# Rewriting the edges of a graph layer behind 60 plain groups instead of 100

## The chip, the cores and the metric

The kernel runs on one core of a Trainium2 chip. The metric is the device time of one execution in microseconds (us). The core has five engines that matter here: PE (TensorE, matmuls), DVE (VectorE), ACT (ScalarE), POOL (GpSimd, which issues the indirect gathers) and SP (SyncE, which issues the plain DMAs). Each runs its own instructions in order, and semaphores make one wait for another.

## The reference

It is one layer of a graph network on 50000 nodes and 1650000 directed edges, sorted by destination `dst`; 50000 of the edges are self loops. Each node has 160 numbers (64 scalars, 32 vectors of 3), each edge four weights. Cut to what matters:

```python
ss, vv = s[src], v[src]                       # gather of x rows by source
out0, out1 = products of (ss, vv) with edge weights e0, e1 and W1 to W5
m_agg = jax.ops.segment_sum(m, dst, num_segments=n)
h  = concatenate([m_agg[:, :64] @ Ws * LIN_S, einsum('nui,uw->nwi', m_agg_v, Wv) * LIN_V])
x  = layernorm(x + (x + relu(h)))
```

As everything up to the relu is linear in the gathered rows, the kernel sums `weight k of the edge × gathered row` by destination first, for k = 0 to 3, and multiplies the sums by combined matrices after.

## The kernel before

**Groups and pairs.** Edges are taken 128 at a time (a unit), 6 units to a group (G = 6), two groups to a pair (PG = 2), 20 groups (SG), so ten pairs, to a load. There are 2087 groups, in 1044 pairs and 105 loads.

**What a pair does.** POOL gathers 12 × 128 rows of `x` into one of four `xg` buffers (line 319; the pool is opened with `bufs=4`). DVE writes `hot` (line 328: which of 32 destinations each edge has, as 0 and 1) and `ha` (line 331: `hot` times each of the four weights). PE multiplies (line 343, `ps`), and DVE transposes the result in 32 × 32 squares (line 349, `sums`). Every two pairs, PE multiplies by the weights (line 579, `phc`) and ACT copies the result out (line 581, `hp`). For each block of 128 nodes PE adds up the groups that touch it (line 639, `phb`), and the node's own term is made (lines 615 to 629: `xt` read at 592, the self loop's weights `sa` read at 596, `ptx`, `xT`, `yx`, `t`). Lines 184 to 199 are the layer norm, 735 sends `out`.

**What a load does.** `load(s)` is called at every tenth pair for the next ten: the plain one reads `src` and `dst` (`ri`) and the weights (`ra`) on SP (lines 260 to 262). One pair later ACT casts them (line 269). Four pairs later `place(s)` (lines 284 to 311) works out where each group begins (`first`, `baseB`), transposes the indices and the weights on PE (lines 285 to 301) and writes `si` (line 303, what the gathers read), `rel` and, in PSUM, `pk` (what `ha` reads).

**Rewriting.** The first HEAD groups are read plainly, self loops with them. For all later edges the self loops are taken out of the stream first, since the node's own term needs no gather. That is done in packs: a pack holds 128 rows of 790 edges, and is a list of 128 steps (function `pack`, some of them empty): read the rows (SP, lines 419 to 423, 2.4 MB), cast them (ACT, lines 427 to 429 and 447), count and mark the self loops and examine the marks (DVE, lines 448 to 493), then two series of shifts by powers of two with predicated copies (DVE, lines 504 to 511, each in two half rows): one gathers the weights of the self loops in `pra`, then lines 523 to 528 pick and collect them into `mine`; the other closes the gaps in the rows, `prow`. Last, SP puts the rows into DRAM one by one (line 563, one DMA of 18.5 KB to `edges` and one of 0.5 KB to `selves` a row). Later loads read from `edges` (line 254, `r6`, 360 KB), and `sa` comes from `selves`.

**What sets the order.** SP's instructions keep the order in which the program is written (`manual_schedule` for SP). Those of the other engines are arranged by a scheduler when the program is built, and are then fixed. A pack's steps are dealt out over the pairs, so that it is done `(first - 1) * per - 1` pairs in, where `first` is the first load that needs its rows and `per` is 10:

```python
todo = math.ceil(len(packs[0]) * min(1, (p + 1 - began) / max(1, due[0] - began)))
```

Pack 0 begins at pair 2 (START). With HEAD = 100 it is due at pair 39; the next ones at 99, 159 and 229. There are 16 packs.

Of the kernel before, what the change touches and what calls it, by code (L numbers as in the profile page):

```python
# [67 lines left out]
SG = 20  # L68

HELP = {}  # L70
HEAD = 100
RP = 128
RS = 16
KM = 31
# [4 lines left out]
def plan(n_nodes, n_edges):  # L79
# [9 lines left out]
                if g == 1 or (g + 0.2) * per_unit + 1 + 5 * math.sqrt(g * per_unit * per_unit / P) <= W)  # L89
    head = math.ceil(min(HEAD, n_edges / (group * P)) / SG) * SG  # L90
    eh = head * group * P
# [917 lines left out]
```

## Time and profile before

| | |
|---|---|
| median of 3 runs | 15705.15 us (15704.62 to 15706.36) |
| the profiled execution | 15737.51 us, span 15735.7 us |
| POOL busy | 11891.8 us, 76% |
| PE busy | 8152.5 us, 52% |
| DVE busy | 6035.6 us, 38% |
| first gather, last gather start | 9.82 us, 15716.99 us |
| mean granted TensorE clock | 0.73 |

How to read it: an engine's busy time leaves out the issuing of DMAs and the handling of semaphores, so a POOL that does nothing but gathers has 76%; the rest stands as "issue" in its waits. A group of instructions reads "line engine operation output<-inputs, shape, count | busy us, mean ns of one | idle time of the engine just before them, and what ended it". A timeline row has start and duration in us, engine (SPq is the queue of SP), line, operation, names and, in square brackets, an idle time before and what ended it. DVE rows that don't wait for one another overlap slightly in the records.

Some times of pairs in that execution, in us from the start of the span:

| pair | gathers, first start to last end | transpose (line 349) |
|---|---|---|
| 14 | 233.95 to 248.67 | 255.85 |
| 15 | 248.98 to 263.69 | 288.30 |
| 16 | 264.00 to 278.71 | 302.15 |
| 19 | 309.09 to 323.81 | 332.12 |
| 20 | 324.11 to 338.86 | 348.69 |
| 46 | 715.07 to 729.80 | 763.85 |

Pair 30's first gather starts at 474.52, pair 50's at 775.23.

### The profile page before, as it was taken

Reading aid. Unit: us, or ns where it says so; the run is one execution under the profiler, and the core shown is the slowest. Engines: PE = TensorE matmul, PEld = TensorE weight load, DVE = VectorE, ACT = ScalarE, POOL = GpSimd, SP = SyncE. Lnnn points to the kernel's source line nnn. Section 1 sums busy time; section 2 is a strip of 40 time slices with the busy share of each in tenths; the row PEclk is TensorE's granted clock in tenths of the full one; section 3 lists DMA queues with packets and bytes.
Section 4 is the critical chain, followed back from the end, with each engine's and each line's share of the span. In section 5 each row is a group of like instructions: output and inputs, shape, how many; then the busy total and the mean of one; then the engine's idle time right before and its main releaser. Section 6 shows DMA issues by size and latency. Waiting matters only on the chain. (4 is left out here: it accounts for less than half of the span.)

```text
span 15735.7 us, 122013 instructions
## 1 busy us (share of the span) xinstructions
PE 8152.5 (52%) x38505; PEld 7452.0 (47%) x38506; DVE 6035.6 (38%) x11070; ACT 499.5 (3%) x1392; POOL 11891.8 (76%) x12536
## 2 busy tenths in 40 slices
PE   4554545555455555555455554554545555455555
PEld 4444545444454444444444444454444444444444
DVE  5342524325253342533425343352433425234222
ACT  0000000000000000000000000000000000000000
POOL 7777777777777777777777777777777777777777
PEclk7777777777777777777777776777777777777777
DMA  3323333233233323333233332332333332332232
GB/s 79 84 74 84 75 76 80 74 82 75 76 80 77 80 75 76 80 78 79 73 79 78 77 81 74 83 75 75 80 76 81 75 82 73 76 79 73 73 75 68
DMA packets 806901, 1215.93 MB, mean 77 GB/s; under 512 B 280851, under 2 KB 585160, under 8 KB 802278
## 3 DMA queue, kind: packets, MB, share of 16 engines
q0 software_dynamic: 601056, 1026.60, 26.6%
q1 hardware_dynamic: 203770, 180.19, 3.9%
q8 instruction: 323, 5.29, 0.1%
q14 instruction: 312, 2.56, 0.1%
q10 hardware_dynamic: 1440, 1.29, 0.0%
HBM read 1135.77 MB, written 71.40 MB: 77 GB/s over the span
## 5 line engine op out<-in xcount | busy, mean ns | idle before, releaser
L319 POOL DMA_INDIRECT xg<-in_x,si x12522 | 11887.6, 949 | 3825.5 <-issue 3777.2
L343 PE MATMUL ps<-xg,ha 128*128 128x160 f32 x25044 | 5686.4, 408 | 7298.0 <-DMA xg<-in_x,si 5676.0
L343 PEld LDWEIGHTS ps<-xg,ha 128*128 128x128 f32 x25044 | 5451.3, 281 | 7580.6 <-issue 6593.5
L349 DVE STREAM_TRANSPOSE sums<-ps 128x320 f32<-128x320 f32 x1044 | 530.7, 512 | 6311.9 <-PE ps L343 6240.0
L331 DVE TENSOR_TENSOR ha<-hot,pk 128x1536 f32<-128x1536 f32 x1044 | 1802.6, 1730 | 206.3 <-PE ps L343 206.3
L627 DVE TENSOR_SCALAR t<-yx,sa 128x160 f32<-128x160 f32 x391 | 147.5, 377 | 2585.8 <-PE yx L623 2585.5
L623 PE MATMUL yx<-BWh,xT 80*128 80x320 f32 x3128 | 1032.0, 472 | 156.6 <-ACT xT L617 152.7
L579 PE MATMUL phc<-BWk,sums 128*128 128x160 f32 x5220 | 820.6, 305 | 22.2 <-DVE t L629 19.7
L623 PEld LDWEIGHTS yx<-BWh,xT 80*128 80x128 f32 x3128 | 599.3, 202 | 439.2 <-ACT xT L617 237.4
L579 PEld LDWEIGHTS phc<-BWk,sums 128*128 128x128 f32 x5220 | 750.7, 193 | 49.6 <-issue 40.3
L639 PE MATMUL phb<-hp,hot 128*128 128x160 f32 x3474 | 562.0, 307 | 6.1 <-DVE t L629 4.3
L328 DVE TENSOR_TENSOR hot<-bank,rel 128x384 f32<-128x384 f32 x1044 | 551.1, 540 | 0.1
L639 PEld LDWEIGHTS phb<-hp,hot 128*128 128x128 f32 x3474 | 503.1, 194 | 60.5 <-issue 50.4
L629 DVE SCALAR_TENSOR_TENSOR t<-yx,sa,t 128x160 f32<-128x160 f32 x1173 | 442.6, 377 | 82.4 <-PE yx L623 67.8
L511 DVE COPY_PREDICATED prow<-marks,prow 128x2370 f32<-128x2370 int32 (+8 forms) x160 | 442.5, 2765 | 0.0
L617 ACT COPY xT<-ptx 80x256 f32<-80x256 f32 x391 | 143.8, 368 | 8133.7 <-PE ptx L615 8133.3
L581 ACT COPY hp<-phc 128x160 f32<-128x160 f32 x522 | 150.3, 288 | 5316.5 <-PE phc L579 5284.5
L511 DVE COPY_PREDICATED pra<-marks,pra 128x1580 f32<-128x1580 int32 (+8 forms) x160 | 304.5, 1903 | 0.0
L605 DVE TENSOR_TENSOR hot<-bank,rr 128x512 f32<-128x512 f32 (+2 forms) x391 | 285.3, 730 | 0.0
L640 DVE TENSOR_TENSOR phb<-phb,t 128x160 f32<-128x160 f32 x391 | 127.4, 326 | 136.1 <-PE phb L639 134.4
L615 PE MATMUL ptx<-ident,xt 128*80 128x128 f32 (+1 forms) x782 | 154.5, 278 | 38.4 <-ACT hp L581 34.1
L193 ACT ACTIVATE rstd<-mv,eps_t 128x1 f32<-128x1 f32 x391 | 115.2, 295 | 1707.3 <-DVE mv L188 1630.5
(144 smaller groups left out, 2600.6 us busy)
## 6 DMA issues: line engine op xcount, KB each, us to landing
xg<-in_x,si POOLq DMA_INDIRECT x12522
edges<-prow SPq DMA_DIRECT2D x1994, 18.5 KB
r<-edges SPq DMA_DIRECT2D x99, 360.0 KB
selves<-mine SPq DMA_DIRECT2D x1992, 0.5 KB
xt<-in_x SPq DMA_DIRECT2D x390, 80.0 KB
out<-o SPq DMA_DIRECT2D x390, 80.0 KB
pra<-in_attr SPq DMA_DIRECT2D x15, 1580.0 KB
sa<-selves SPq DMA_DIRECT2D x390, 2.0 KB
```

The source lines that it names most:

```text
L319: got.append(nc.gpsimd.indirect_dma_start(out=xg[:, j, :], out_offset=None, in_=x, in_offset=bass.IndirectOffsetOnAxis(ap=placed[0][:, u + ...
L328: nc.vector.tensor_tensor(hot[:, :n], slotsP[:, 0:W].unsqueeze(1).to_broadcast([P, n, W]), rel[:, u:u + n].unsqueeze(2).to_broadcast([P, n ...
L331: nc.vector.tensor_tensor(ha[:, :n], hot[:, :n].unsqueeze(2).to_broadcast([P, n, NK, W]), pk[:, :, u:u + n].rearrange("p k u -> p u k").un ...
L343: mm = nc.tensor.matmul(ps[:, j // G, :], ha[:, j].rearrange("p k w -> p (k w)"), xr, start=j % G == 0, stop=j % G == G - 1)
L349: nc.vector.transpose(at[:, :, i:i + ng, :].rearrange("p b g w -> p g b w"), ps[:, :ng].rearrange("p g (b f) -> p g b f", f=FB))
L511: nc.vector.copy_predicated(what[:n, a:e], mi[:, r].unsqueeze(2).to_broadcast([n, e - a, what.shape[2]]), what[:n, a + d:e + d])
L579: nc.tensor.matmul(ph[:ng * W], at[:, b, :ng].rearrange("p g w -> p (g w)"), BWk[:, b, :], start=b == 0, stop=b == ND - 1)
L605: nc.vector.tensor_tensor(hot2[:, :len(cs)], slotsP.unsqueeze(1).to_broadcast([P, len(cs), P]), rr[:, :len(cs)].unsqueeze(2).to_broadcast( ...
L615: nc.tensor.transpose(pt[:, i, :nb], xt[:nb, i * H:(i + 1) * H], ident[:nb, :nb])
L623: nc.tensor.matmul(y[:nb], xT[:, i, :nb], BWh[:, i, ks, :], start=i == 0, stop=i == 1)
L629: nc.vector.scalar_tensor_tensor(t[:nb], y[:nb, i], sa[:nb, k:k + 1], t[:nb], op0=ALU.mult, op1=ALU.add)
L639: nc.tensor.matmul(ph[:nb], hot2[:r, i, :nb], hp[:r], start=i == 0, stop=i == len(cs) - 1)
```

## The change

The constant HEAD goes from 100 to 60.

```diff
-HEAD = 100
+HEAD = 60
```

With it `plan()` gives 60 plain groups instead of 100, so three plain loads instead of five and 102 `r6` loads instead of 100; 2033 rows to rewrite instead of 1994, still in 16 packs; 2086 groups instead of 2087, so 12516 gathers instead of 12522 (the self loops of the plain groups are gathered with the rest: about 46080/33 = 1396 instead of 76800/33 = 2327). Pack 0 is due at pair 19 instead of 39 and has 18 pairs instead of 38; the next ones are due at pairs 79, 139 and 209. Line 563 makes 4319 DMAs instead of 4236.

In the order of the built program, DVE's instructions are the same up to the transpose of pair 14. In the program before, the half-steps of pack 0's shifts then alternate with the `hot`, `ha` and transposes of pairs 15 to 22. In the changed one, all that is left of pack 0 at the transpose of pair 15 (the end of the first series of shifts, lines 523 to 528, the second series) follows that transpose without anything between, and `place(2)` and the `ha` of pair 16 come after it. On SP, `load(2)` (lines 260 to 262) stood ahead of pack 0's puts and now stands behind the first 16 of them, which is where `load(3)` stood. `place(3)` reads an `r6`, which stands on SP behind all of pack 0's puts and behind pack 1's reads, and on DVE behind the first half of pack 1's count (lines 448 to 469).

## The prediction

> **What bounds the kernel now.** I read the page first, then POOL's waits, then the DVE, SP and PE timelines around the first pack. From the page:
>
> ```profile
> span 15735.7 us, 122013 instructions
> ...
> L319 POOL DMA_INDIRECT xg<-in_x,si x12522 | 11887.6, 949 | 3825.5 <-issue 3777.2
> ```
>
> 12522 gathers with 0.949 us of work and 0.30 us of issue each make 1.2528 us apiece, 15688 of the 15736 us. POOL's waits, as us in total, times, longest:
>
> ```profile
> POOL xg L319 <- issue: 3777.2, 12389, 0.4
> POOL xg L319 <- DMA xg<-in_x,si: 17.4, 53, 0.8
> POOL xg L319 <- DVE rel L306: 6.8, 1, 6.8
> ```
>
> So nothing in the body stops POOL: time is the number of gathers by 1.2528, plus any stall of POOL. It has four `xg` buffers, so the gather of pair p+4 waits for the last matmul of pair p (line 343), and that waits for pair p's `ha` on DVE (331). What counts is whether DVE can leave that chain alone.
>
> In DVE's timeline pack 0's steps now alternate with the chain (start, us, instruction):
>
> ```profile
> 305.69 0.58 DVE L509 COPY_PREDICATED pri<-marks,pri 128x395 int32<-128x395 int32 x1
> 306.17 2.86 DVE L511 COPY_PREDICATED prow<-marks,prow 128x2370 f32<-128x2370 int32 x1
> 308.93 0.50 DVE L349 STREAM_TRANSPOSE sums<-ps 128x320 f32<-128x320 f32 x1
> 309.36 0.54 DVE L504 TENSOR_SCALAR marks<-pri 128x395 int32<-128x395 int32 x1
> ...
> 361.68 2.67 DVE L511 COPY_PREDICATED prow<-marks,prow 128x2274 f32<-128x2274 int32 x1
> ```
>
> The last L511 ends at 364.35; SP, which waited for it, then puts the rows out, with the next plain load behind 16 puts:
>
> ```profile
> 133.00 0.40 SPq L260 DMA_DIRECT2D ri<-in_src  x1
> ...
> 364.42 0.30 SPq L563 DMA_DIRECT2D edges<-prow  x1
> ...
> 370.77 0.35 SPq L260 DMA_DIRECT2D ri<-in_src  x1
> 371.18 0.43 SPq L261 DMA_DIRECT2D ri<-in_dst  x1
> 372.03 0.32 SPq L262 DMA_DIRECT2D ra<-in_attr  x1
> ```
>
> The load at 133.00 is that of groups 40 to 59 (pairs 20 on), the one at 370.77 that of pairs 30 on.
>
> **The change, part by part.**
>
> *Gathers.* The plan gives 2086 groups instead of 2087: 12516 gathers, 6 fewer by 1.2528, −7.5 us. The tail after the last gather (15716.99 to 15735.7, 18.7 us) stays.
>
> *Other counts.* Two plain loads become `r6` loads; 39 more rows are put (83 more SP DMAs of 0.23 us, over 16 packs); the packs' casts and DVE steps stay 16 times. POOL issues none of these; later packs keep 60 or 70 pairs each. Nothing for these, while SP's longest put stretch, priced below, stays ahead.
>
> *Pack 0 in 18 pairs instead of 38.* Its 128 steps go out 7.1 a pair instead of 3.4, and the built order shows where: up to the transpose of pair 14 DVE's order is that of before; after the transpose of pair 15 comes the rest of pack 0 in one block (three half-steps of the `pra` shift, L523/L525 twice, L528, ten half-steps of `prow`, the last two short), with no `hot`, `ha` or transpose between. Only then come `place(2)` (L284 on) and the `ha` of pair 16. On SP, load(2) now stands behind pack 0's first 16 puts, so behind the block's last L511. Before, it went at 133.00.
>
> The block starts when pair 15's matmuls end:
>
> ```profile
> 265.44 6.26 PE L343 MATMUL ps<-xg,ha 128*128 128x160 f32 x24 [8.54 <-DMA xg<-in_x,si]
> ...
> 286.29 6.08 PE L343 MATMUL ps<-xg,ha 128*128 128x160 f32 x24 [12.41 <-DVE ha L331]
> ...
> 297.31 2.88 PE L343 MATMUL ps<-xg,ha 128*128 128x160 f32 x20
> ```
>
> 271.7, with the transpose 272.2. Its length: a `prow` half-step is L504 0.56, L506 0.55, L508 0.64, L509 0.58, L511 2.77. In the trace dependent neighbours start 0.04 after the end of the one before (L186 to L188, 698.63 + 0.33 to 698.99) and independent ones 0.1 before it (L509 to L511, 306.17). That makes 5.15; a `pra` half-step with L511 at 1.88 makes 4.3. Sum: 3 × 4.3, two picks 4.8 (0.55 + 1.78 each), L528 5.6, 8 × 5.15 = 41.2, last two 6.9: 71.4 us, to 343.6. If all neighbours overlap as in the interleaved stretch it is 65.
>
> Then (tE = the block's end), by before's rows after 364.35: puts from tE+0.07, `ri` at +6.4 and +6.8, `ra` at +7.7; its packets end at 374.0 and 375.1 (+9.7 and +10.8). From there the place(6) stretch is the pattern:
>
> ```profile
> 586.00 0.27 DVE L284 TENSOR_SCALAR first<-starts,rf 120x20 f32<-120x20 f32 x1
> ...
> 589.29 1.74 DVE L331 TENSOR_TENSOR ha<-hot,pk 128x1536 f32<-128x1536 f32 x1
> ...
> 596.72 0.52 DVE L349 STREAM_TRANSPOSE sums<-ps 128x320 f32<-128x320 f32 x1 [1.43 <-PE ps L343]
> ```
>
> ACT's cast (L269) at 585.56 to the matmuls' end at 596.7 is 11.1 us. Pair 16 is done near tE + 9.7 + 11.1 ≈ tE+21, 364.6. Pair 20's gather, which started at 324.11, starts there: a stall of 40.5 us. Pairs 17 to 19 are gathered by then, 3.4 us of matmul each, and the old pace returns. This wait also holds pair 16's `hot`, `ha`, transposes, own terms and `out` behind it; none reaches POOL except through pair 20.
>
> What the trace can't show is a block alone on DVE and matmuls after 80 us of idle PE. Bounds: block 65 to 71.4 (I take 71.4, the dependent row, as each instruction of the order waits for its neighbour); matmuls 3.4 (764.70, warm) to 6.1 (286.29, after idle); I take 5.6. Low end 40.5 − 6.4 − 2.2 ≈ 32; high 41.
>
> Row against rule: PEclk is 0.50 over 126 to 138 us and 1.00 over 138 to 144. The Trainium skill ("TensorE: Matmul & The Clock Gate", Part 1, "What's actually happening") says one idle window of some 3.4 us halves the clock and some 3.4 us of work restores it, so it would price pair 16 at 3.4 cold plus about 1.7 warm, 5.1 us: 0.5 less than my row, and the sum 0.5 lower.
>
> *SP's puts and pair 30.* Pack 0's 17 groups of 16 put DMAs run without a pause from 343.7, with `out` and `xt` between. Before, the first group with the load took 9.3 us (364.42 to 373.75), one alone 7.9 (to 381.63), one with `out` or `xt` some 8.7, the last, short one 5.3 (605.46 to 610.75): 9.3 + 9 × 7.9 + 6 × 8.7 + 5.3 = 138, to 482. Behind them pack 1's 2.4 MB and then `r6` for pair 30: before, that pack's load was issued at 612.16 and landed at 621.8, so `r6` lands near 494. Pack 1's count (L448 to L469 from about 490, 6.6 us as at 732.51) stands ahead of L284 on DVE: 496.6; ten more us to the `ha` of pair 26 (739.07 on, less its `yx` waits), then 3.4 to 6: done at 510.5 to 513. Pair 30's gather is due at 474.52 + 40.5 = 515.0. Margin 2 to 4.5 us, so nothing; the cover is thin, and past it each us is a us of stall.
>
> **Sum**: +40.5 − 7.5 = +33. The profiled execution took 15737.5 (span 15735.7), 32 above the median of 15705.15, without a cause that I can name; its pace of gathers is 0.2% slower, which moves a stall of 40 us by 0.1. After's span on that footing 15769; predicted median 15705 + 33 = 15738.
>
> **Rivals.**
>
> *A, the buffers cover it (the other side).* If pair 16 is done by 324.1, POOL sees nothing: −7.5, 15698. Price: block plus 21 us against 52 (324.1 − 272.2), so no stall needs a block under 31 us, and a block under 38 us breaks even. For it: four buffers hide every wait in the trace. Against: the block's 13 L511, two L525 and L528 alone sum to 42 us.
>
> *B, a second wait at pair 30.* If all puts run at 8.8 us a group (381.63 to 390.47) or `r6` lands late behind the 2.4 MB, pair 26 is 3 to 20 us later and the margin goes: +36 to +55, 15741 to 15760. For: the margin of only 2 to 4.5. Against: pair 46 before, the same place one pack later, was done at 763.85 with its buffer needed at 775.23, 11 us early.
>
> *C, a shorter stall.* Block at the interleaved pace and warm matmuls: 32 − 7.5, so +24 to +28, 15729 to 15733. For: 361.68 to 364.25 shows overlap at work. Against: the waits in the order.
>
> *D, the order is not what runs.* The order is fixed at build, so only data readiness can differ; a gain beyond A has no source.
>
> **How the numbers follow.** 0.2% of 15705, 31.4 us, is about what a measurement here can tell from no change. Forecast (+28 to +36) 0.47, B 0.25, C 0.20, A 0.05, other 0.03. Slower by over 0.2%: B whole, 0.65 of the forecast, a little of other: 0.57. Faster by over 0.2% needs −31 where only 7.5 is to be had: 0.02. Same: 0.41. Range: 15724 (C's end less 5, for a landing or a matmul quicker than any row here) to 15760 (B's end); A is left out.
>
> **What would show it.** In the changed profile: one POOL wait of about 40 us ahead of pair 20's first gather, near 324; DVE from 272 to 344 in L504 to L528 alone; load(2) issued near 350; puts from 344 to 482; no POOL wait near 515; 12516 gathers at 1.25 us. No wait near 324 makes A right; a second one near 515, B; 32 us at the first, C. I am wrong if POOL's pace itself changes (0.2% of it is as much as the whole effect) or the stall is over 60 us.

## The result and the profile after

The changed kernel takes 15747.44 us (median of 10 runs, 15745.27 to 15748.56); before, timed with it, takes 15705.85 us (10 runs, 15703.89 to 15706.82). That is +41.6 us, a ratio of 1.0026 [1.0018, 1.0035]: slower, by a little more than the 31.4 us (0.2%) that the prediction held a measurement to tell from no change; the interval's lower end is just under that. The forecast was 15738, +33.

The profiled execution took 15747.3 us. Its span, gathers and POOL's waits (us in total, times, longest):

```profile
span 15745.5 us, 122127 instructions
...
L319 POOL DMA_INDIRECT xg<-in_x,si x12516 | 11847.6, 947 | 3871.1 <-issue 3768.1
```

```profile
POOL xg L319 <- issue: 3768.1, 12369, 0.3
POOL xg L319 <- PE ps L343: 40.7, 5, 39.4
POOL xg L319 <- DMA xg<-in_x,si: 34.4, 73, 1.4
```

There is one long wait of POOL, 39.4 us for a matmul, which before did not have. The waits for DMA are 34.4 us instead of 17.4, which nobody forecast. The long one is at pair 20's first gather; the row above it in POOL's timeline is pair 19's last:

```profile
322.76 0.94 POOL L319 DMA_INDIRECT xg<-in_x,si  x1 [0.30 <-issue]
363.14 0.94 POOL L319 DMA_INDIRECT xg<-in_x,si  x1 [39.44 <-PE ps L343]
```

What pair 16's matmuls wait for is seen in DVE's timeline:

```profile
270.74 0.52 DVE L349 STREAM_TRANSPOSE sums<-ps 128x320 f32<-128x320 f32 x1 [9.32 <-PE ps L343]
271.18 0.55 DVE L504 TENSOR_SCALAR marks<-hit 128x395 int32<-128x395 int32 x1
...
339.96 2.67 DVE L511 COPY_PREDICATED prow<-marks,prow 128x2274 f32<-128x2274 int32 x1
352.05 0.23 DVE L284 TENSOR_SCALAR first<-starts,rf 120x20 f32<-120x20 f32 x1 [9.42 <-ACT rf L269]
...
362.91 0.52 DVE L349 STREAM_TRANSPOSE sums<-ps 128x320 f32<-128x320 f32 x1 [1.11 <-PE ps L343]
```

Pair 15's transpose, the block of pack 0 from 271.18 to 342.63 with nothing of a pair in it, 9.42 us in which DVE has nothing to do, then `place(2)` and pair 16's transpose. The idle 9.42 us are spent on the load of pair 20's groups, which SP could only issue after the block, in SP's timeline:

```profile
342.70 0.30 SPq L563 DMA_DIRECT2D edges<-prow  x1
...
348.27 0.34 SPq L260 DMA_DIRECT2D ri<-in_src  x1
348.66 0.40 SPq L261 DMA_DIRECT2D ri<-in_dst  x1
349.11 0.41 SPq L262 DMA_DIRECT2D ra<-in_attr  x1
```

Where the 41.6 us lie, from the two profiled executions (the place ahead of each number):

| where | us |
|---|---|
| wait at pair 20's first gather, 39.44 instead of 0.30 | +39.1 |
| 6 gathers fewer, at 1.250 us (0.947 + 0.30) | −7.5 |
| time lost by POOL from pair 900 on, 12.1 instead of 7.2 | +4.9 |
| from the last gather's start to the end, 15722.60 to 15745.5 instead of 15716.99 to 15735.7 | +4.2 |
| first gather, at 10.22 instead of 9.82 | +0.4 |
| sum | +41.1 |

The two executions differ by only 9.8 us, since that of before ran 32 us above its own median: its gathers took 1.2527 us each, and those of the changed kernel 1.2503. Over 12516 gathers this is 30 us, and it is no part of the change: the table's rows are differences of waits, not of starts.

The +4.9 comes from the last pack. SP issues the reads of its rows like this:

```profile
13687.27 17.72 SPq L422 DMA_DIRECT2D pri<-in_dst  x1
13705.03 12.36 SPq L423 DMA_DIRECT2D pra<-in_attr  x1
```

and while the packets of `pra`, one of 12640 bytes a row, move, from 13719.25 to 13782.99, gathers have to wait for theirs, for instance

```profile
13749.75 0.94 POOL L319 DMA_INDIRECT xg<-in_x,si  x1 [1.39 <-DMA xg<-in_x,si]
```

Before, the last pack held 1994 − 15 × 128 = 74 rows, and its packets of `pra` took 20.9 us (13990.08 to 14010.98). Now it holds 2033 − 15 × 128 = 113, and they take 63.7 us, 22 GB/s. A pack of 128 rows, more than either, takes 5.1 to 7.1 us in the two executions. (Of before's 7.2 us, 4.8 are one slow gather, told of in the last section; the last read thus costs 12.1 us now and at most 2.4 before.)

The +4.2 is in the chain of work that ended last. Before:

```profile
15716.99 4.43 DMA xg<-in_x,si
...
15721.45 0.55 PE ps L343 x2
...
15722.43 1.60 PE phc L579 x10
15724.03 1.10 PE phb L639 x8
```

and after:

```profile
15722.60 5.22 DMA xg<-in_x,si
...
15727.86 0.90 PE ps L343 x2
15728.76 1.60 PE phb L639 x6
15730.36 3.43 PE phc L579 x20
15733.79 2.62 PE phb L639 x14
```

2087 groups left one group in the last pair; 2086 leave two, and 20 instead of 10 weight multiplies (579) and 20 instead of 8 sums over groups (639) come after the last gather has landed.

### The profile page after: what moved, and what is told of

It reads as the page before. It is cut to its first block, busy times and chain, and to the rows that moved or that the text cites. A ratio compares the mean times of both kernels' runs of the same rounds, so it can differ in the third digit from the quotient of the medians.

```text
span 15745.5 us, 122127 instructions
## 1 busy us (share of the span) xinstructions
PE 8150.1 (52%) x38497; PEld 7448.5 (47%) x38498; DVE 6047.3 (38%) x11067; ACT 498.8 (3%) x1390; POOL 11851.8 (75%) x12530
## 5 line engine op out<-in xcount | busy, mean ns | idle before, releaser
L511 DVE COPY_PREDICATED prow<-marks,prow 128x2370 f32<-128x2370 int32 (+8 forms) x160 | 442.5, 2765 | 0.1
L511 DVE COPY_PREDICATED pra<-marks,pra 128x1580 f32<-128x1580 int32 (+8 forms) x160 | 305.0, 1907 | 0.0
L605 DVE TENSOR_TENSOR hot<-bank,rr 128x512 f32<-128x512 f32 (+3 forms) x391 | 286.5, 733 | 0.1
```

What stands on the lines that cost most here:

```text
L511: nc.vector.copy_predicated(what[:n, a:e], mi[:, r].unsqueeze(2).to_broadcast([n, e - a, what.shape[2]]), what[:n, a + d:e + d])
L605: nc.vector.tensor_tensor(hot2[:, :len(cs)], slotsP.unsqueeze(1).to_broadcast([P, len(cs), P]), rr[:, :len(cs)].unsqueeze(2).to_broadcast( ...
```

## The experiments

The theory: pack 0's block and, behind it on SP, `load(2)` make the wait at pair 20; its length is the block and some 20 us more, less 52 us that the buffers cover. The main rival: that 18 pairs are simply too few, so that the denser steps delay DVE wherever the load stands. Further open: which lock is next if the buffers are made more, and whether the shape of the last pack costs anything.

The twelve runs, of seven kernels, came in four groups, each on one chip with the kernel before beside it. On three of these chips before itself took 19476 to 19626 us, and in the profiles taken there PE is held back (the last section); totals are compared within a group only, and what a wait does is read from the traces.

**The load put ahead of the puts.** Four empty steps in pack 0 shift its first put behind `load(2)` in SP's order; 60 groups, 18 pairs and all the work stay. DVE's built order changes with it: there is no block between the transposes of pairs 15 and 16 any more, and pack 0's half-steps alternate with pairs 15 to 19.

```diff
             steps += [None, None]
             steps += [None, None]
+            if c == 0:
+                steps += [None] * 4
```

> 60 plain groups, with four empty steps ahead of pack 0's puts, so that load(2) stands on SP ahead of them, as load(2) and load(3) stood with 100. In the built order pack 0's shifts alternate with the ha of pairs 16 to 23 again. Queue theory (the block and the wait at pair 20 come from load(2) standing behind a put that waits for the whole pack; 18 pairs are also too few for the puts): no wait at pair 20; pack 0 ends near 372 us instead of 343, its puts near 509, r6 lands near 521, pair 26 is done near 538 and pair 30's gather, due at 474, waits some 64 us. Time 15747 + 25 = 15772. Rival (only the place of load(2) is at fault): no wait anywhere, 15747 - 39 = 15708. Rival (the density of 7.1 steps a pair alone makes the wait): the wait at pair 20 stays, 15747.

> The kernel of e1_load_ahead again (60 plain groups, load(2) on SP ahead of pack 0's puts), on a chip where PE is not held up. Queue theory: no wait at pair 20; pack 0 ends near 372 us, its puts near 509, r6 lands near 521, pair 26 is done near 538, and pair 30's gather, due at 474, waits some 64 us; 15747 + 25 = 15772. Rival (only the place of load(2) is at fault): no wait anywhere, 15747 - 39 = 15708. Rival (the density of the steps alone): a wait at pair 20 as after has it.

> The kernel of e1_load_ahead and e5_load_ahead, for the chip of the last call, where PE is not held up (before at 15707). Queue theory: no wait at pair 20; pack 0 ends near 372 us, its puts near 509, r6 lands near 521, pair 26 is done near 538, pair 30's gather, due at 474, waits some 64 us: 15747 + 25 = 15772. Rival (only the place of load(2) is at fault): no wait anywhere, 15747 - 39 = 15708. Rival (the density of the steps alone): a wait at pair 20 as after has it, 15747.

It ran in three groups, each time on a chip with PE held back: 19715.07 against 19626.1 (1.0050 [1.0033, 1.0067]), 19584.83 against 19475.77 (1.0052 [1.0035, 1.0069]) and 19715.63 against 19611.87 (1.0069 [1.0044, 1.0094]). POOL's timeline in the first, at pair 20 and at pair 30:

```profile
372.76 0.95 POOL L319 DMA_INDIRECT xg<-in_x,si  x1 [0.30 <-issue]
...
667.00 1.00 POOL L319 DMA_INDIRECT xg<-in_x,si  x1 [98.64 <-PE ps L343]
```

The wait at pair 20 is gone in all three; it is 78.6 us in the kernel with the load behind the puts, in the same group (below). So the density of the steps alone does not make this wait, and that rival falls for pair 20: the place of one load does, together with the order that is built from it (the edit moves both, and no run parts them). But much of the time is then waited for later: 34.2, 34.5 and 34.2 us at pair 26 and 98.6, 96.0 and 96.7 us at pair 30, where pair 30's own load stands behind all of pack 0's puts. The wait at pair 26 is the same lock with the next read in `load(2)`'s place. After the last `ha` before pack 0's end, at 444.44, the shifts run alone to 471.17, and `xt`, which an own term needs, stands on SP behind the puts that wait for them. From SP's and PE's timelines in the first group (in this kernel the lines from 539 on stand 2 further down):

```profile
471.24 0.28 SPq L565 DMA_DIRECT2D edges<-prow  x1
...
486.98 0.38 SPq L594 DMA_DIRECT2D xt<-in_x  x1
```

```profile
489.82 0.62 PE L617 MATMUL ptx<-ident,xt 128*80 128x128 f32 x2 [54.30 <-DMA xt<-in_x]
```

Pair 22's matmuls come behind this `ptx` on PE; its transpose is at 504.20, and pair 26's gather starts at 504.44. In the first group the waits at pairs 26 and 30 are together 53.8 us more than the same two in the other kernel (9.4 and 69.6), of the 78.3 that were saved. In total it is 52.0 us below that kernel (19767.07), where 24.5 are left of these waits; the rest was not followed up. Against before it is still 0.5 to 0.7% slower, so that 18 pairs cost time even with `load(2)` ahead is not refuted. How long pair 30 would wait on a chip whose PE is not held back was not measured.

**A shorter block.** Pack 0 leaves out the first two of its five `prow` shifts, four half-steps (the rows are then not closed up); empty steps keep everything else in place.

```diff
-                for b in range(bits):
+                for b in range(2 if c == 0 and far == "far" else 0, bits):
...
-                steps += [partial(next, g, None)] * (4 * KM.bit_length() - (0 if all_ else 2))
+                steps += [partial(next, g, None)] * (4 * KM.bit_length() - (0 if all_ else 10 if c == 0 else 2))
+                steps += [None] * (8 if c == 0 and not all_ else 0)
```

> 60 plain groups; pack 0 leaves out the first two of five shifts of prow, four half-steps of 5.2 us, so its rows are not closed up rightly. Block theory (the wait is block + 20.3 us less 52): block 71.4 - 20.9 = 50.5, wait at pair 20 of 39.1 - 20.9 = 18.2 us, all after it earlier by as much: 15747 - 21 = 15726. Rival (the wait is set by SP's puts and the load, not by DVE): wait and time as they are, 15747.

> The kernel of e2_short_pack again: 60 plain groups, pack 0 without the first two of five shifts of prow (four half-steps of 5.2 us; its rows are not closed up rightly). Block theory: block 50.5 us, wait at pair 20 of 39.1 - 20.9 = 18.2 us, 15726. Rival (the wait is set by SP's puts and the load): 39 us, 15747.

In the first group its total is 19724.47 against 19626.1 (1.0059 [1.0042, 1.0075]), in the second 19587.46 against 19475.77 (1.0057 [1.0040, 1.0074]). The totals say little, as pair 30's waits of 69.2 and 74.4 us, and PE's pace after them, are in them. The wait itself, in the first group:

```profile
433.42 0.94 POOL L319 DMA_INDIRECT xg<-in_x,si  x1 [56.92 <-PE ps L343]
```

78.62 − 56.92 = 21.7 us less than with the whole block in the same group, where the four half-steps were priced at 20.9. The block itself, from its first L504 to its last L511, is 50.5 us instead of 71.4, so 20.9 less: within 0.8 us, each microsecond of block was a microsecond of wait. In the second group the wait is 46.06 us, with no run with the whole block and four buffers beside it. The length of the wait depends also on how late POOL already is when it begins; the time from the end of pair 15's transpose to pair 20's first gather hardly does. It is 91.9, 93.0 and 92.5 us with the whole block (the changed kernel, the one with the read in two pieces in the first group, and the same where PE keeps its pace), and 71.3 and 70.8 us with the short one.

**A fifth buffer.**

```diff
-tc.tile_pool(name="rows", bufs=4) as rowp
+tc.tile_pool(name="rows", bufs=5) as rowp
```

> 60 plain groups, five xg buffers instead of four. If the wait at pair 20 is for the buffer alone, one more covers a further pair: the wait moves to pair 21 and is 39.1 - 15.0 = 24 us, 15732. If pair 20's own si is also late, as the place(2) at 352.05 to 354.85 suggests, pair 20 waits for that, to 354.9: 30.9 us, 8.2 less, 15739. In before the spare buffer would bring nothing.

> The kernel of e3_five_buffers again: 60 plain groups, five xg buffers. If the wait at pair 20 is for a buffer alone: it moves to pair 21 and is 39.1 - 15.0 = 24 us, 15732. If pair 20's si (ready near 354.9) holds it next: 30.9 us at pair 20, 15739.

19378.89 against 19626.1 (0.9874 [0.9858, 0.9891]) and 19232.28 against 19475.77 (0.9876 [0.9846, 0.9905]). These totals are a gain only on chips where PE is late throughout; they say nothing on the others. At pair 20 the wait is still there, and its releaser is another one. DVE's and POOL's timelines in the first:

```profile
459.08 0.28 DVE L303 TENSOR_SCALAR si<-bank 128x120 int32<-128x120 f32 x1 [0.23 <-issue]
459.28 0.27 DVE L306 SCALAR_TENSOR_TENSOR rel<-bank,baseB 128x120 f32<-128x120 f32 x1
```

```profile
459.63 0.95 POOL L319 DMA_INDIRECT xg<-in_x,si  x1 [88.39 <-DVE rel L306]
```

No buffer is waited for here, but the indices `si` of pair 20, which `place(2)` writes, which waits for the same `load(2)`. From the end of pair 15's transpose to that gather it is 83.6 us, and 93.0 in the kernel with four buffers in the same group: 9.4 less, where 8.2 was expected (83.7 in the second group). So behind the lock of the four buffers stands the next, less than 10 us of wait away.

**Fifth buffer and shorter block together.** Both diffs above.

> 60 plain groups, pack 0 without the first two of five shifts of prow (20.9 us less block; its rows are not closed up rightly), and five xg buffers. Block theory with si as the next lock: si(2), written at 354.8 in after, comes at 333.9, pair 20 waits some 10 us, no wait at pair 21: 15747 - 29 = 15718. If the buffer alone is the lock: no wait at pair 20, 18.2 - 15.0 = 3 us at pair 21, 15711. If the block's length does not set it: 31 us at pair 20, 15739.

19376.99 against 19611.87 (0.9895 [0.9871, 0.9919]).

```profile
439.22 0.94 POOL L319 DMA_INDIRECT xg<-in_x,si  x1 [67.95 <-DVE rel L306]
```

The wait is 88.39 − 67.95 = 20.4 us shorter than with the whole block, though on another chip; with the whole block it was 88.39 and 87.5 us on two chips. From the end of pair 15's transpose to pair 20's first gather it is 63.1 us, against 83.6 and 83.7. So the block sets this second lock one for one too.

**The last read in two pieces.** The reads of a pack (lines 419 to 423) are made in two, the first of a multiple of 16 rows, so 112 and 1 instead of 113.

```diff
+                m = n // 16 * 16
+                for r, q in ((0, m), (m, n)):
+                    if r == q:
+                        continue
+                    e = slice(e0 + r * L, e0 + q * L)
-                dq.dma_start(pri[:n, 0, :L], src1[e].rearrange("(r e) o -> r (e o)", e=L))
+                    dq.dma_start(pri[r:q, 0, :L], src1[e].rearrange("(r e) o -> r (e o)", e=L))
...
-                dq.dma_start(pra[:n, :L].rearrange("r e k -> r (e k)"), attr[e].rearrange("(r e) k -> r (e k)", e=L))
+                    dq.dma_start(pra[r:q, :L].rearrange("r e k -> r (e k)"),
+                                 attr[e].rearrange("(r e) k -> r (e k)", e=L))
```

> 60 plain groups; a pack's reads of pri and pra go out in two pieces, the first of a multiple of 16 rows. Only the last pack differs: 113 rows become 112 and 1. Theory: the read of 113 rows is what slowed the gathers of pairs 911 to 913 by 12.1 us (its 12640 byte packets came one each 0.56 us from 13719.25 to 13782.99, those of 128 rows one each 0.045 us); with 112 + 1 rows it lands within some 8 us and the gathers keep their 1.25 us: 15747 - 11 = 15736. Rival (the slow stretch is a matter of the place in the data or of the moment): it stays, 15747.

> The kernel of e4_even_read again: 60 plain groups, a pack's reads in two pieces. Theory: the slow stretch of 12.1 us at the last pack's read goes (that read took 63.8 us from first to last packet with 113 rows and 6.5 with 112 + 1 in the runs before this one); where PE is not held up 15747 - 11 = 15736, wait at pair 20 as in after, 39 us. Rival (the slow stretch belongs to the place in the data): 15747.

The first of them, in the first group, took 19767.07 against 19626.1 (1.0075 [1.0058, 1.0092]). Its two waits are those that the other kernels of that group are set against:

```profile
451.39 0.94 POOL L319 DMA_INDIRECT xg<-in_x,si  x1 [78.62 <-PE ps L343]
...
694.58 0.94 POOL L319 DMA_INDIRECT xg<-in_x,si  x1 [69.59 <-PE ps L343]
```

The packets of its last read take 7.0 us from the first one's start to the last one's end, and 64.3 to 65.2 us where the read is whole in that group. The second ran on a chip where before takes 15706.85: 15736.62 us (15735.54 to 15738.43), ratio 1.0019 [1.0009, 1.0029], where 15736 was expected. SP's reads of the last pack, and POOL there and at pair 20:

```profile
13684.01 0.42 SPq L427 DMA_DIRECT2D pri<-in_dst  x1
13684.48 0.43 SPq L428 DMA_DIRECT2D pra<-in_attr  x1
```

```profile
364.08 0.94 POOL L319 DMA_INDIRECT xg<-in_x,si  x1 [41.09 <-PE ps L343]
...
13749.92 0.94 POOL L319 DMA_INDIRECT xg<-in_x,si  x1 [0.30 <-issue]
```

SP issues in 0.43 us what took 12.36, no gather waits there, and pairs 911 to 913 lose less than 0.1 us instead of 12.1. They gather the same rows as in the changed kernel, so the place in the data is not the cause. The total is 15747.44 − 15736.62 = 10.8 us below the changed kernel, of another chip, with befores 1.0 us apart. The wait at pair 20 is as long as ever, so the slow read is a term by itself.

**80 groups, with the read in two pieces.** HEAD = 80 gives pack 0 28 pairs, half of the step between the two kernels; at first with four buffers.

```diff
-HEAD = 60
+HEAD = 80
```

> 80 plain groups, and each pack's reads in two pieces, the first of a multiple of 16 rows (the last pack has 93 rows: 80 and 13). Pack 0 has 28 pairs, its puts begin near 380 us, load(3) stands behind half of them, near 447, and pair 26 is done near 463, ahead of pair 30's need at 474.5. Theory: no wait at pairs 20 to 40; 12516 gathers as with 60 groups, 7.5 us less than before; a tail after the last gather of 23 us instead of 18.7 (an even number of groups, the last pair whole), +4.2; no slow stretch in the last pack's read, -6.6 against before: 15706 - 10 = 15696. Rival (a pack in fewer than 38 pairs always stops POOL): a wait of some 20 us, 15716 or more.

19481.88 against 19475.77, 1.0002 [0.9991, 1.0014]. At pair 20 4.4 us are left, but pairs 30 and 40 wait 56.3 and 39.2 us on this chip; that no pair would wait on a chip with PE at its pace was not shown by it.

**80 groups, read in two pieces, five buffers.**

> 80 plain groups, five xg buffers, reads of a pack in two pieces. Where PE is not held up (before at 15706): no wait at pairs 20 to 40, 12516 gathers (-7.5), tail +4.2, last read -6.6: 15696, the fifth buffer brings nothing. Where PE is held up in stretches (before at 19480 to 19630): the fifth buffer covers one more pair of each stretch, as in e7_five_buffers (1.2% under before although that kernel has the waits at pairs 20 and 30); without those waits some 0.5% more, 1.6 to 1.8% under before.

On the chip where before takes 15706.85 (15705.41 to 15710.98), it takes 15698.75 us (15696.31 to 15700.70), where 15696 was expected: 8.1 us less, with no run of the one within the runs of the other, but a ratio of 0.9994 [0.9985, 1.0004], which is no difference by the bound of 31.4 us. It is the fastest kernel here, by an amount that these runs can't vouch for. POOL's waits:

```profile
POOL xg L319 <- issue: 3784.5, 12422, 0.6
POOL xg L319 <- DMA xg<-in_x,si: 15.7, 43, 2.1
```

But for the first gather's 7.3 us for its indices, which before has too (6.8), there is no wait for a matmul or an index left. Its pack 0 was slower than expected (last shift done at 407.05, not 380; `load(3)` at 465.75, not 447): pair 26's transpose starts at 482.57, and pair 30's first gather went at 476.32. With four buffers it would have waited some 6 us (an estimate from these two rows); the fifth covers it.

## Why the prediction was right, and where it was not

The forecast was +40.5 − 7.5 = +33; measured +41.6. That is inside the range of 15724 to 15760, but above the +28 to +36 that the forecast itself covered, in the band set for rival B, whose second wait did not come: in this part the range held by luck. Step by step:

| step | predicted | measured |
|---|---|---|
| block of pack 0 | 71.4 us | 71.45 (271.18 to 342.63) |
| its end tE | 343.6 | 342.63; it began 1.0 sooner, as pair 15's matmuls took 5.24 us instead of 6.26 |
| `ri` of `load(2)` issued | tE + 6.4 and 6.8 | tE + 5.6 and 6.0 |
| ACT's cast | tE + 9.7 | tE + 9.0 |
| pair 16's matmuls | 5.6 us | 5.2 |
| pair 16 done | tE + 21 | tE + 20.2 |
| wait at pair 20 | 40.5 us | 39.4, so 39.1 more than before |
| six gathers | −7.5 | −7.5 |
| pack 0's puts end | 482 | 477.5 |
| margin at pair 30 | 2 to 4.5 us | 4.0 |

The cast is in ACT's timeline, the matmuls that set the margin in PE's:

```profile
351.61 0.40 ACT L269 CAST rf<-ri 120x256 f32<-120x256 int32 x1 [104.91 <-DMA ri<-in_dst]
```

```profile
503.53 5.68 PE L343 MATMUL ps<-xg,ha 128*128 128x160 f32 x24 [4.54 <-DVE ha L331]
```

Pair 26 is done at 503.53 + 5.68 = 509.2, and pair 30's first gather went at 513.22 with no wait. Rival A (the buffers cover the block) was refuted by the wait itself, rival B (a second wait at pair 30) by this margin. That the lock of B is real was seen on the chips where PE is late: there pair 30 waited 69 to 99 us with 60 plain groups and four buffers. Rival C (a shorter block) fell with 71.45 us; the value from neighbours that wait for each other was the right one, and the 65 us of the interleaved pace was not. Rival D (another order than the built one) has nothing for it: the instructions of the table came in the built order. Two figures of the prediction do not come out of their terms. B's upper end of +55 is 2 us more than 33 + 20, and does not take off the margin; the range's end of 15760 rests on it. And 0.949 + 0.30 us make 1.249 us a gather; 1.2528 is the pace from pair to pair, which moves the six gathers by 0.02 us.

Pair 16's matmuls took 357.64 to 362.87, 5.2 us, after 82 us in which PE was idle and 5 us with only the few matmuls of `place(2)`. The row of before gave 5.6. The Trainium skill ("TensorE: Matmul & The Clock Gate", Part 1, "What's actually happening") would have given 5.1: the rule was nearer.

The sum lacks 8.6 us. Two steps failed, with +4.9 and +4.2 in the table of the result; the wait at pair 20 was 1.4 under its forecast, the first gather 0.4 late, and 0.5 is in no row.

The first is "Other counts", of which the prediction says "Nothing for these": "39 more rows are put" was followed to the puts, but not to the read of the last pack, whose number of rows went from 74 to 113. Its time hangs on the number itself: 128 rows 5.1 to 7.1 us, 74 rows 20.9, 113 rows 63.7, and 112 and 1 in two pieces 7.0 and 8.8. That the odd read costs the time was shown by splitting it and nothing else (less than 0.1 us of waits instead of 12.1). Which DMA engine takes a packet is not in the trace, but how many packets move at a time is: their own times add up to 56.3 us within the 63.7 with 113 rows (0.9 at a time), to 36.7 within the 20.9 with 74 (1.8), and to 75.6 within 6.4 with the 128 rows of pack 1 (11.8). The rates go with it: 22 GB/s with 113 rows, twice that with 74 (74 × 12640 bytes in 20.9 us is 44.8), some 250 in that pack of 128.

The Trainium skill ("DMA: Bandwidth & Descriptors", "Why a DMA increments its semaphore by 16 and not by 1") has a rule for this: a transfer is spread over the largest number of engines up to 16 that divides the slowest dimension of both its sides. That makes 16 for 128 rows, 2 for 74 and 1 for 113. The trace agrees for 74 and 113 (1.8 and 0.9 packets at a time, 2 to 1 in the rates); 128 rows have 11.8 at a time and some 11 times the rate of 113. It was the rule that spoke against this change, and the prediction did not weigh it.

The second is "The tail after the last gather … stays": it was taken from before's 18.7 us without asking what the last pair holds. With 2086 groups it holds two instead of one, and the tail is 22.9 us. This was read from the two chains and not tried by itself. The two other kernels that ran where PE keeps its pace also have 12516 gathers, so 2086 groups, and theirs is 23.74 us (60 plain groups) and 21.33 us (80): longer than before's 18.7 too, but by 5.0 and 2.6 us, so +4.2 is good to some 2 us.

So the mechanism was right, and its price to 1.4 us; the error of +9.1 lies in two places at the other end of the program, both set by a remainder that the constant changed.

## What to carry to other kernels

A load for work that is due soon must not stand, on a queue that keeps its order, behind a store that waits for a long stretch of another engine: the engine that is to be fed then waits for that whole stretch, and more buffers only move the lock from the rows to their indices. To move one load ahead is not enough either: here the next read behind the same store (`xt`) took its place. A constant that moves a boundary moves every remainder behind it as well, so work out what the last piece, the last pair and the last read hold, before pricing them at nothing. Where the rows of a DMA are no multiple of 16, read a multiple of 16 of them first and the rest in a second piece: here, with 113 rows, that took 12 us of waits to nothing.

## What the runs showed of the hardware that was not expected

On three of the four chips of the experiments PE is held back: it stands idle between single matmuls, and no wait that the profile shows explains it. From PE's timeline of the kernel with the read in two pieces, in the first group:

```profile
310.95 0.42 PE L343 MATMUL ps<-xg,ha 128*128 128x160 f32 x1 [1.20 <-issue]
313.75 0.42 PE L343 MATMUL ps<-xg,ha 128*128 128x160 f32 x1 [2.38 <-issue]
315.85 0.42 PE L343 MATMUL ps<-xg,ha 128*128 128x160 f32 x1 [1.68 <-issue]
```

Such idle times of over 0.4 us within the 24 matmuls of one pair stand 1387 times in that trace, 2.2 ms in all, and not once in that of the same kernel on the fourth chip. The whole program takes 24 to 25% longer there (before: 19476 to 19626 instead of 15706 us), POOL waits for buffers and is no longer the bound, and with a fifth buffer the kernel with 60 plain groups takes 1.2% less than before; on the fourth chip that kernel did not run. The mean granted clock is 0.66 instead of 0.73. The cause is open.

In before, one gather took 5.72 us instead of 0.95, beside an L528 over the 74 rows of the last pack:

```profile
14264.67 5.72 POOL L319 DMA_INDIRECT xg<-in_x,si  x1 [0.30 <-issue]
```

```profile
14263.89 5.58 DVE L528 TENSOR_REDUCE mine<-pra 74x128 f32<-74x3200 f32 x1
```

No gather was held beside the same line over 128, 113 or 93 rows. It is 4.8 of the 7.2 us that before loses in its last stretch. It was seen once, in one execution; whether the number of rows has to do with it is open.
